# A gated RNN and a GRU on one core: VectorE's bank reads and additions, spread three by three over the half steps

## The chip, the cores and the metric

The kernel runs on one core of one Trainium2 chip. The metric is the device time of one execution in microseconds (us), lower is better. Engines are named as in the profile: PE is TensorE (matmul), PEld its weight loads, DVE is VectorE, ACT is ScalarE, POOL is GpSimd and SP is SyncE, which issues the DMAs.

## The reference, cut to what matters

Two layers, each added to its input `x` of shape (64, 128, 512): 64 sequences of 128 steps and 512 features. Layer 0 is a recurrence that can be written with cumulative sums and is computed as such; the change doesn't touch it. Layer 1 is a GRU with a condition vector per sequence:

```python
vz, vr, vh = video @ C_z + b_z, video @ C_r + b_r, video @ C + b
xz, xr, xh = seq @ W_z, seq @ W_r, seq @ W        # for all steps at once
def step(h, ...):                                  # 128 times, one after the other
    z = sigmoid(xz_t + h @ U_z + vz)
    r = sigmoid(xr_t + h @ U_r + vr)
    hh = tanh(xh_t + r * h @ U + vh)               # (r * h) @ U
    h = (1.0 - z) * h + z * hh
x = x + all h
```

Everything is float32.

## The kernel before, in words

**Layer 0** (the first 690 us or so) goes over 16 groups of four sequences and four blocks of 128 features. It is limited by its matmuls (L232).

**Layer 1** splits the 64 sequences into two *streams* of 32 (`st0`, `st1`) that take turns, so that the matmuls of one stream lie beside the sigmoid, tanh and products of the other. One time step of one stream is a *half step*: the generator `Stream.halves`, driven by `take(n)` along the list `order`. Its parts, in the order of issue:

1. `h` times U_r and U_z (32 PE instructions, L464, `g<-w_s,h`), into the PSUM bank `g`, which already holds the step's x-share.
2. ACT: sigmoid to `r` (L918). DVE, by halves: `rh = r * h` (L922) and its transposition (L923), twice each. ACT: sigmoid to `z` (L927). POOL: `1 - z` (L933) and `(1 - z) * h` (L934).
3. The *middle*: up to two outer products on PE (below), up to three sums on POOL (L810), and on DVE **reads of banks** (`read`), then the deferred transposition of an output (L994).
4. `rh` times U (L464, `g<-w_s,fi`), after that further outer products up to a goal, ACT's tanh (L957), and ACT's copy of the next x-share into `g` (L871).
5. DVE: `hh * z` (L969), plus `(1 - z) * h` (L970), transposition of the new `h` (L974). POOL: `h + x` for the output (L985).
6. The **end** of the half step: one addition of x-sums (`add_c`) and `reads[1]` further reads; SP loads the x-share of two steps later, if it is stored.

**The x-shares** (x times W_z, W_r, W plus the condition) are not computed step by step. For eight time steps of both streams together, a *group*, the products are done by Strassen's scheme in two levels: seven `Outer` operands, each with seven products, 49 products a group, which the planner spreads over 16 half steps (`place`, with `GOALS`). A product is 8 PE instructions (L602). Its banks in PSUM are `r11`, `r12a`/`r12b` (by turns), `r21`, `r22` and `shared`. Within an operand the contents are handed on from bank to bank by ACT (`continued`, L615: r11 to r12, r12 to r21, r21 to r22; L626 copies `shared` to SBUF), and each finished bank is *read* by DVE: `read` adds it to a sum in SBUF (L704, `W<-r,W`); for r12 and r22 the common part is added first in place (L699, `r<-r,x`), as a read of its own. The banks wait in the list `to_read`. An operand gives six reads, a group 42.

Where an operand's sum must still be added to another one, this goes to DVE for operand 4 (`add_c`, L719, `W<-W`, four a group, waiting in `to_add_c`) and to POOL for operand 5 (`add`, L724, four a group). After that SP stores the shares to DRAM (`to_store`, L732) at the beginning of the next half step, and loads them by step and stream (`load_share`, L865).

A product or copy that would overwrite a bank that is not yet read calls `free`, which issues the missing reads first. `read` of operand 5 issues a missing addition of its block first (L694). Instructions marked `pin` stay in program order on their engine, so the order in which `read` and `add_c` are called is the order on DVE; each engine works through its list in order.

How many reads a half step takes is `reads`, which `take` hands over: (2, 2) at the two places where a stream catches up, (4, 1) while the layer fills up, (0, 2) in the last steps, and **(4, 0)** in all half steps between. The middle then takes `max(4, len(to_read) - 2)` reads, as far as there are any; the end takes one addition and no read:

```python
read(reads[0] and max(reads[0], len(to_read) - 2))     # L942, middle
...
add_c()                                                  # L1002, end
read(reads[1])                                           # L1003
```

Of the kernel before, what the change touches and what calls it, by code (L numbers as in the profile page):

```python
# [19 lines left out]
def kernel(  # L20
# [58 lines left out]
    def pin(instruction):  # L79
        return tc.keep_in_program_order(instruction)  # L80
# [484 lines left out]
    class Outer:  # L565
# [121 lines left out]
        def read(self, block, common):  # L687


            (m, j), n, r = block, self.n, self.bank(block)  # L690

            while n in (0, 5) and (m, j) in waiting:
                add(1)
            while n == 5 and (m, j) in waiting_c:  # L694
                add_c()
            if j == 1 and not common:
                if not hasattr(self, "common"):
                    shared_to_copy[0]()
                pin(nc.vector.tensor_tensor(r, r, self.common, ALU.add))  # L699
                return  # L700
            u, s5, c = (acc[:, i, m, j] for i in range(3))
            v1, v21 = v_x[:, j], v_x[:, 2 + j]
            dst, other = ((u, v1), (c, u), (u, u), (s5, v21), (c, s5), (u, u), (c, u))[n]
            pin(nc.vector.tensor_tensor(dst, r, other, ALU.add))  # L704
            unread.discard(r.name)
            if n == 1:
                self.store(c, 0, m, j)
            elif n == 4:
                waiting_c.add((m, j))
                to_add_c.append(lambda: self.add_c(c, u, m, j))  # L710
            elif n == 5:
                waiting.add((m, j))
                to_add.append(lambda: self.add(s5, u, m, j))
            elif n == 6:
                self.store(c, 1, m, j)

        def add_c(self, c, u, m, j):
            waiting_c.remove((m, j))
            pin(nc.vector.tensor_tensor(c, c, u, ALU.add))  # L719
            self.store(c, 0, m, 2 + j)  # L720

        def add(self, s5, u, m, j):
            waiting.remove((m, j))
            pin(nc.gpsimd.tensor_tensor(s5, s5, u, ALU.add))  # L724
            self.store(s5, 1, m, 2 + j)
# [14 lines left out]
    to_read, unread = [], set()  # L740
    to_add, waiting = [], set()
    to_add_c, waiting_c = [], set()
# [23 lines left out]
    def sum_tasks(group):  # L766
# [24 lines left out]
        def halves(d):  # L791
            *ts, op = d
            return [(*[t[:, k] for t in ts], op) for k in range(HC)]

        outer = [
            [(base - 1, ("s", group, i, k), d_) for k, d_ in enumerate(halves(d))]
            for i, d in enumerate(wsums(x_[0][0], x_[0][1], x_[1][0], x_[1][1], s_))
        ]
# [37 lines left out]
    class Stream:  # L836
# [56 lines left out]
        def halves(self, t, filler=None, between=None, targets=lambda: (0, 0), busy=False, reads=(4, 0)):  # L893
# [45 lines left out]
            place(targets()[0], busy)  # L939
            if filler:  # L940
                filler()
            read(reads[0] and max(reads[0], len(to_read) - 2))  # L942
            while deferred:
                deferred.pop(0)()
            if between:
# [52 lines left out]
            if APART <= t + AHEAD < S:  # L998

                pin(nc.gpsimd.tensor_copy(ident.rearrange("p (k b) -> p k b", b=SB), x_of(self, t + AHEAD)))  # L1000
                deferred.append(lambda: pin(nc.vector.transpose(self.output(t + AHEAD), ident)))
            add_c()  # L1002
            read(reads[1])  # L1003
            if t + 2 < S and not direct(self, t + 2) and all((t + 2, q) in stored for q in range(Q)):
                self.load_share(t + 2)
# [226 lines left out]
    for t in range(LEAD + 1, S):  # L1232
        n = order[-1][1] + 1
# [74 lines left out]
    n = 0  # L1308
# [44 lines left out]
```

## Time and profile before

| | |
|---|---|
| time, three runs | 1876.83, 1877.01, 1879.24 us; median 1877.01 |
| profiled execution | 1878.12 us, of it a span of 1876.3 us |
| granted TensorE clock | 0.999 |
| busy in the span | PE 99%, PEld 56%, DVE 80%, POOL 46%, ACT 39% |
| DVE from 1200 to 1600 us | 152 of each 200 us |
| bank reads L704, 128x384 | 0.54 us each |
| additions L719, 128x384 | 60, shortest 0.514, median 0.517, longest 1.050 us |
| output sums L985 | 0.50 us each, waiting mostly for L974 |

A row of a timeline or of the chain has the start in us from the span's start, the length in us, and what it is: engine, line of the kernel, operation, the tile written and the tiles read, and the shape. "x8" says that so many instructions with the same names were merged. In brackets stands how long the engine was idle before, and what ended it. A group of matmuls that has started and waits for its next weights still counts as busy.

### The profile page before, as it was taken

The numbers are of one execution on the slowest core, as the hardware profiler recorded it, in microseconds if no ns is written. First come the engines' busy times: TensorE is split into PE (matmuls) and PEld (weight loads), VectorE is DVE, ScalarE is ACT, GpSimd is POOL, SyncE is SP. The second block draws the span as 40 slices with busy tenths as digits, with TensorE's granted clock in tenths as the row PEclk, the third lists the DMA queues.
The fourth block names the chain that finished last, engine by engine and source line by source line (L and its number), as shares of the span: only waits on it lengthen the run. The fifth ranks groups of instructions, "written<-read, shape, count | busy, mean of one in ns | idle before, by whom it ended". The sixth has DMA issues, their size and how long they took to land.

```text
span 1876.3 us, 62311 instructions
## 1 busy us (share of the span) xinstructions
PE 1864.2 (99%) x24793; PEld 1054.2 (56%) x24793; DVE 1504.9 (80%) x3438; ACT 722.6 (39%) x1888; POOL 865.1 (46%) x1544
## 2 busy tenths in 40 slices
PE   9999999999999999999999999999999999999998
PEld 5444444444444445566666666666666666666567
DVE  5899999999999976777777777777777777777786
ACT  3232223222232233344444444444444444444434
POOL 1233232333333344546556556466565565565650
PEclk9999999999999999999999999999999999999999
DMA  7765433444333241334334344344343343443343
GB/s 181 176 124 119 82 70 73 88 82 83 73 76 65 49 86 29 101 90 142 112 101 142 94 115 133 104 124 126 96 137 109 99 141 101 114 130 96 111 111 78
DMA packets 366754, 195.38 MB, mean 104 GB/s; under 512 B 225332, under 2 KB 352064, under 8 KB 366464
## 3 DMA queue, kind: packets, MB, share of 16 engines
q1 hardware_dynamic: 366280, 191.33, 40.9%
q8 instruction: 195, 3.19, 0.7%
q14 instruction: 95, 0.78, 0.1%
q10 hardware_dynamic: 184, 0.07, 0.0%
HBM read 78.63 MB, written 81.13 MB: 85 GB/s over the span
## 4 chain that ended last, share of the span: by engine, by line
PE 98%; DVE 1%; issue 0%; DMA 0%; ACT 0%; SPq 0%; DVEq 0%; ACTq 0%
PE g L464 36%; PE p L232 35%; PE r L602 14%; PE r12a L602 4%; PE shared L602 4%; PE r12b L602 4%; PE gz L464 1%; PE tp L190 0%; PE pv L464 0%; DMA x<-in_x_dram 0%; DVE W L704 0%; PE g_first L464 0%; DVE fi L923 0%; DVE fi L922 0%; DVE r L339 0%
## 5 line engine op out<-in xcount | busy, mean ns | idle before, releaser
L232 PE MATMUL p<-xT,W 128*128 128x512 f32 (+1 forms) x1560 | 661.9, 586 | 0.0
L232 PEld LDWEIGHTS p<-xT,W 128*128 128x128 f32 x1560 | 293.5, 190 | 361.6 <-issue 359.1
L464 PE MATMUL g<-w_s,h 128*32 128x256 f32 (+1 forms) x8128 | 481.0, 373 | 2.3 <-issue 1.6
L464 PEld LDWEIGHTS g<-w_s,h 128*32 128x32 f32 x8128 | 301.4, 110 | 179.4 <-issue 83.2
L464 PEld LDWEIGHTS g<-w_s,fi 128*32 128x32 f32 x8128 | 222.7, 109 | 113.9 <-issue 55.4
L464 PE MATMUL g<-w_s,fi 128*32 128x128 f32 x8128 | 276.3, 273 | 2.7 <-DVE fi L922 1.3
L922 DVE TENSOR_TENSOR fi<-fi,h 128x64 f32<-128x64 f32 (+1 forms) x494 | 112.3, 227 | 179.3 <-ACT fi L918 178.5
L985 POOL TENSOR_TENSOR h<-h,x 128x128 f32<-128x128 f32 x242 | 121.3, 501 | 232.4 <-DVE h L974 206.8
L314 POOL COPY first<-condT 128x4 f32<-128x4 f32 x64 | 12.6, 196 | 461.8 <-DVE h L386 432.8
L918 ACT ACTIVATE fi<-g 128x128 f32<-128x128 f32 x254 | 70.6, 278 | 327.7 <-PE g L464 308.9
L933 POOL TENSOR_SCALAR fi<-fi 128x128 f32<-128x128 f32 x240 | 72.6, 302 | 236.6 <-DVE fi L922 226.5
L704 DVE TENSOR_TENSOR W<-r,W 128x384 f32<-128x384 f32 x315 | 169.2, 539 | 7.4
L310 ACT ACTIVATE fi<-fi 128x512 f32<-128x512 f32 x64 | 40.4, 631 | 340.6 <-DVE fi L351 340.6
L957 ACT ACTIVATE h<-g 128x128 f32<-128x128 f32 x255 | 70.9, 278 | 236.2 <-PE g L464 236.2
L923 DVE STREAM_TRANSPOSE fi<-fi 128x64 f32<-128x64 f32 (+1 forms) x494 | 122.2, 247 | 22.8 <-PE r12a L602 0.5
L969 DVE TENSOR_TENSOR h<-h,fi 128x128 f32<-128x128 f32 (+1 forms) x264 | 94.9, 359 | 43.8 <-ACT h L957 43.1
L253 POOL TENSOR_TENSOR x<-xT,h 128x512 f32<-128x512 f32 x63 | 122.6, 1946 | 4.9
L934 POOL TENSOR_TENSOR fi<-fi,h 128x128 f32<-128x128 f32 x240 | 110.8, 462 | 20.0
L970 DVE TENSOR_TENSOR h<-h,fi 128x128 f32<-128x128 f32 (+1 forms) x264 | 97.7, 370 | 27.2 <-POOL held L810 0.9
L810 POOL TENSOR_TENSOR held<-held 128x128 f32<-128x128 f32 x240 | 113.7, 488 | 3.1
L602 PE MATMUL r<-w_inner,held 128*32 128x384 f32 x1080 | 114.6, 486 | 0.0
L339 DVE RECIPROCAL r<-r 128x256 f32<-128x256 f32 x60 | 104.2, 1737 | 0.0
(158 smaller groups left out, 2721.5 us busy)
## 6 DMA issues: line engine op xcount, KB each, us to landing
shares<-W SPq DMA_DIRECT2D x240, 192.0 KB, 2.1
xz<-shares SPq DMA_DIRECT2D x480, 48.0 KB, 1.9
whole_v<-shares SPq DMA_DIRECT2D x480, 48.0 KB, 2.0
x2d<-x SPq DMA_DIRECT2D x63, 256.0 KB, 4.2
words<-held SPq DMA_DIRECT2D x240, 64.0 KB, 2.1
out_dram<-o SPq DMA_DIRECT2D x240, 64.0 KB, 1.8
xw_None<-x2d SPq DMA_DIRECT2D x56, 256.0 KB, 3.4
w_rows<-in_L_cond_W_f_dram SPq DMA_DIRECT2D x4, 256.0 KB, 5.7
```

What stands on the lines that cost most here:

```text
L232: nc.tensor.matmul(p[:, tokens], lhsT=W0[:, c, n, k, :], rhs=xT[g][:, k, tokens], start=(k == 0), stop=(k == K - 1),)
L253: nc.gpsimd.tensor_tensor(x2.rearrange("p (t b) -> p t b", b=GB)[:, ts], xT[g][:, c, :].rearrange(f"{layout(g)} -> p t b", b=GB)[:, ts], b ...
L339: pin(nc.vector.reciprocal(r, r))
L464: nc.tensor.matmul(p[q * SB : (q + 1) * SB], lhsT=lhsT(k), rhs=part(wk, q), start=(start and k == 0), stop=(stop and k == len(w) - 1), ski ...
L602: nc.tensor.matmul(self.bank(bank)[q * SB : (q + 1) * SB], lhsT=a[:, q * SB : (q + 1) * SB], rhs=w_, start=start, stop=True, skip_group_ch ...
L704: pin(nc.vector.tensor_tensor(dst, r, other, ALU.add))
L810: pin(nc.gpsimd.tensor_tensor(*a))
L922: pin(nc.vector.tensor_tensor(rh[:, e], r[:, e], h_[:, e], ALU.mult))
L923: pin(nc.vector.transpose(rhT[:, e], rh[:, e]))
L934: pin(nc.gpsimd.tensor_tensor(r, r, h_, ALU.mult))
L970: pin(nc.vector.tensor_tensor(h[:, e], hh[:, e], r[:, e], ALU.add))
L985: nc.gpsimd.tensor_tensor(hh.rearrange("p (k b) -> p k b", b=SB), hT.rearrange("p (k b) -> p k b", b=SB), x_of(self, t), ALU.add,)
```

## The change

Only half steps with `reads == (4, 0)` change. The middle now takes a fixed number of DVE instructions, three, or four if at least six are waiting in both lists together. An addition of x-sums counts as one of them and is issued first; the rest are reads. The end of these half steps has no addition any more. (An addition that `read` itself forces, for operand 5, is not counted.) Half steps with other `reads` are as before.

```diff
@@ halves, the middle
             if filler:
                 filler()
-            read(reads[0] and max(reads[0], len(to_read) - 2))
+            even = reads == (4, 0)
+            if even:
+                n = 3 if len(to_read) + len(to_add_c) < 6 else 4
+                n -= len(to_add_c[:1])
+                add_c()
+                read(n)
+            else:
+                read(reads[0] and max(reads[0], len(to_read) - 2))
             while deferred:
                 deferred.pop(0)()
@@ halves, the end
-            add_c()
+            if not even:
+                add_c()
             read(reads[1])
```

## The prediction

> **What bounds the kernel now.** First the page. Its last lines here are the chain that ended last, as shares of the span by engine.
>
> ```profile
> span 1876.3 us, 62311 instructions
> ...
> PE 1864.2 (99%) x24793; PEld 1054.2 (56%) x24793; DVE 1504.9 (80%) x3438; ACT 722.6 (39%) x1888; POOL 865.1 (46%) x1544
> ...
> PE 98%; DVE 1%; issue 0%; DMA 0%; ACT 0%; SPq 0%; DVEq 0%; ACTq 0%
> ```
>
> TensorE is the chain. VectorE is 80% busy, but its work can only matter where a matmul waits for it, and such a wait hides inside "busy" PE: the group's row simply gets longer. So the second view is the chain piece by piece (start, length, what), for two half steps of layer 1:
>
> ```profile
> 1168.48 0.65 PE r12b L602 x8
> 1169.12 0.65 PE r L602 x8
> 1169.77 1.05 PE g L464 x32
> ...
> 1173.19 0.65 PE r12b L602 x8
> 1173.83 0.65 PE r L602 x8
> 1174.48 0.87 PE g L464 x32
> ```
>
> A half step is `h` times U_r, U_z (1.73 us), two outer products (0.65 each), `rh` times U (0.87), and one product more (at some places two). Undisturbed it takes 4.536 us (the chain's groups of 1.73 start at 1110.77, 1115.31, ... 1133.45). The 1.05 is 0.18 of waiting for `rhT`. I went through the chain from 795.85 to 1794.19 (216 half steps) and took each half step's length less its parts: 7.9 us of waiting, in 49 half steps; the other 167 wait less than 0.02. **So 7.9 us, 0.42%, is all that any rearrangement of VectorE could bring there.**
>
> Third, the timeline (start, length, engine and line), where a wait arises and where it doesn't:
>
> ```profile
> 1302.40 0.46 POOL L985 TENSOR_TENSOR h<-h,x 128x128 f32<-128x128 f32 x1
> 1302.43 0.51 DVE L922 TENSOR_TENSOR fi<-fi,h 128x64 f32<-128x64 f32 x1 [0.24 <-ACT fi L918]
> ...
> 1311.72 0.23 DVE L922 TENSOR_TENSOR fi<-fi,h 128x64 f32<-128x64 f32 x1 [1.27 <-ACT fi L918]
> ```
>
> VectorE's chain to `rhT` (L922, L923, L922, L923) needs 0.9 us after the sigmoid, in which PE has 1.29 us of products. It comes late when GpSimd's L985 runs at the same moment (0.51 for 0.23), and L985 starts when the previous half step's transposition L974 is done and GpSimd's sums L810 are done. Measured from a half step's start, L922 is due at 6.84 (the next half step's 2.30); L985 (0.46) started at 6.43 costs nothing (857.99 in the timeline), at 6.68 it costs 0.09 (923.10), at 6.80 0.21 (1302.40). If L974 ends after 6.95, L922 itself is late: 7.24 (863.42) costs 0.29. It is a window, and not simply "fewer reads is better".
>
> Waits by what the half step before held (reads are L699/L704, 0.54 each; the addition is L719): four reads with an addition L724 and wide sums on GpSimd, 9 half steps, 2.50 us; three reads with the same GpSimd work, 4, 0.85; four reads with other work, 15, 1.62; reads and an addition behind L974, 8, 0.99; an addition among the reads, 10, 0.64; two products that waited for a read, 1.00; one other, 0.32.
>
> The last but one is the fourth view, the chain at 1141:
>
> ```profile
> 1141.73 0.24 DVE fi L923
> 1141.97 0.98 DVE W L704 x2
> 1142.95 0.04 issue
> 1142.99 0.85 PE r L602 x8
> ```
>
> Bank r11 gets its next product right after `rh` times U; its last read was second in VectorE's row, so PE waited 0.50.
>
> **The change part by part.** It adds and removes no instruction. The order on VectorE is fixed by the code, so I followed the counters (`to_read`, `to_add_c`, products placed) half step by half step; for the kernel before this gives the trace's VectorE order in every half step from 795.85 to 1822. For the changed one, from 832.77 on: mid-half-step work of three instructions in 147 half steps instead of 57, of four or five in 25 instead of 65, of one or two in 38 instead of 88. Each term below is such a count times a price from a row.
>
> *Nine heavy half steps* (four reads before wide sums): seven get three reads. The price is then that of the four rows that already have three reads before the same work, 0.21 (1300.14 is one). 2.50 becomes 7 x 0.21 + 0.53 = 2.00: **-0.5**.
>
> *Four reads with other work*, all to three or two: L974 ends 0.48 earlier, by 6.3, L985 falls before L922: **-1.6** (at least -0.8).
>
> *Additions now ahead of the reads.* L719 leaves the place behind L974 and comes right after L923, beside GpSimd's L933/L934. Nine half steps become L719 and three reads: L974 ends near 6.63, inside the window, at about 0.18 each, 1.6, where 0.99 was lost: **+0.6** (-1.0 to +0.9). Those with an addition already in the middle: **+0.3** (0 to +1). L719's price there:
>
> ```profile
> 919.94 0.46 POOL L934 TENSOR_TENSOR fi<-fi,h 128x128 f32<-128x128 f32 x1
> 920.12 0.70 DVE L719 TENSOR_TENSOR W<-W 128x384 f32<-128x384 f32 x1
> ```
>
> 0.70, against a median of 0.517 for all 60; I take 0.6 to 0.7. The Trainium skill's "SBUF — State Buffer", section "Who interferes with whom", speaks against the new place: a VectorE instruction with two SBUF inputs and a GpSimd one that reads SBUF exclude each other for the whole instruction, while one with a single SBUF input (a bank's read) goes undisturbed. By that rule, as an estimate, L719 could wait out all of L934 and end 0.5 later still, and the total below would be 1 us higher.
>
> *Light half steps filled up.* Ten with L724 and three sums on GpSimd had one or two reads and no wait after them; now they have three instructions, three more a late tanh. GpSimd is busy to 6.4 there and L974 moves from 5.9 to 6.5, so L985 starts at 6.6 to 6.7: 13 x 0.10 = **+1.25** (0, or 13 x 0.21 = 2.7).
>
> *Copies that wait for a postponed read.* A read put off to the next half step delays the ScalarE copy (L615, 0.46) that refills its bank, and in ScalarE's order tanh, L871 and the next sigmoid stand behind it. In four half steps the copy waits for the third or fourth instruction: tanh at 5.4 for 4.2, L974 at 6.7 or later: **+0.7** (0 to 1.2). Where it waits for the second, tanh ends at 5.0, when VectorE is only just done with its reads: nothing.
>
> *Products behind such copies.* The seventh product of an operand adds into r21, which the copy r21 to r22 must have read, and the copy needs r22 read. This meets in one half step three times. At 842.49 the reads ran at
>
> ```profile
> 845.67 0.52 DVE L704 TENSOR_TENSOR W<-r,W 128x384 f32<-128x384 f32 x1
> 846.11 0.56 DVE L699 TENSOR_TENSOR r12a<-r12a,x 128x384 f32<-128x384 f32 x1
> 846.27 0.27 PEld L602 LDWEIGHTS r<-w_inner,held 128*32 128x32 f32 x8
> 846.38 0.86 PE L602 MATMUL r<-w_inner,held 128*32 128x384 f32 x8
> 846.70 0.56 DVE L704 TENSOR_TENSOR W<-r12a,W 128x384 f32<-128x384 f32 x1
> ```
>
> After: the addition, the read of r11, then r22's as third, done at 847.35; copy to 847.86; the product at 847.9, not 846.38: +1.53. At 1379.45 r22's read is second (ends 4.18), copy to 4.68, product at 4.75, not 3.89: +0.86. At 1073.29 a product stands between: +0.19. And the 0.50 at 1138.63 grows by an addition ahead of the two reads, +0.66. Together **+3.2** (2.4 to 4.2).
>
> *Loads and stores.* Additions earlier let their stores go earlier; nobody waits for that. Six loads of x-shares (one a group at most) are issued at a half step's start instead of the end of the one two before. Four issues of 0.45 and 1.9 to land give 3.7, needed by L871 at 4.5, and PE feels nothing before the sigmoid at 6.5: 0, by that slack. The last eight products-thin half steps (1794 to 1822) lose an addition behind L974 and gain reads: 0.
>
> Sum: -0.5 - 1.6 + 0.6 + 0.3 + 1.25 + 0.7 + 3.2 = **+4.0 us**. The profiled execution took 1878.12 (span and 1.8 around it), 1.1 over the median of 1877.01, so it would become 1882.1 and the median **1881.0**.
>
> **Rivals.** (1) *Near nothing*: the window is missed more often than hit and the light half steps stay free, as L985 did up to 6.43: the terms of 1.25, 0.7 and 0.6 fall to about a third, +2: 1879; at the bottom of every bound, 1877. For it: prices at the window's edge go from 0 to 0.2 within 0.2 us. (2) *Faster*: the copies' waits are the mechanism to be removed from the sum; if r22's read came in time (if the product at 842.49 starts within 0.2 of `rh` times U, the sign turns), what is left is -2.1 with light half steps free: 1874.5. Against it: the order on VectorE and the chain at 1141, where just such a wait is seen. (3) *Late loads*: if the six loads land over 6.0 into the half step, ScalarE's order holds up the sigmoid; 1 us each is +6 more, 1887. Against it: 2.3 us of slack; for it: SyncE's queue waits for stores. (4) That the change doesn't do what it says: the callers with empty lists at the first steps do nothing, and the rest does split the work into threes; no chance given.
>
> **How the numbers follow.** Forecast 0.55, four fifths of it over 1880.8; near nothing 0.25; faster 0.10, two thirds of it by over 0.2%; late loads 0.10. 0.2% (3.75 us) is about what a measurement of this kernel can tell from no change. Slower 0.44 + 0.10 = 0.54, faster 0.07, same 0.39. Range: bounds of the terms without all falling on one side, +0.3 to +7: 1877.3 to 1884.0.
>
> **What would show it.** Right: on the chain after, a gap of about 1.5 us near 846 and of 0.9 near 1385 (with the small shift by then), with ACT r L615 and DVE W L704 on it; L719 at 0.6 or more on average and right behind L923; groups of 1.05 to 1.10 in other half steps than now, about as many. Wrong: if the product after 845.5 follows at once, or if the `rh` groups are 0.87 nearly everywhere, the time falls by up to 4 us; if ACT g L871 is seen waiting for DMA for over 1 us, the third rival holds.

## The result and the profile after

| | before | changed |
|---|---|---|
| median, 21 runs each | 1877.83 us | 1879.98 us |
| lowest to highest | 1876.83 to 1879.24 | 1879.03 to 1881.77 |
| profiled execution, its span | 1878.12, 1876.3 | 1881.14, 1879.2 |

The ratio is 1.0013, with a 95% interval from 1.0007 to 1.0019: the change makes the kernel 1.3 to 3.6 us slower. 1881.0 was forecast, 1.0 above the measured median. Against its own 1877.0 the forecast was +4.0, and the medians are 2.15 apart, so a good part of what was forecast did not come.

In the changed kernel the lines behind the middle have moved by seven: L957 is L964, L969 is L976, L970 is L977, L974 is L981, L985 is L992, L994 is L1001. First its page:

```profile
span 1879.2 us, 62306 instructions
...
PE 1864.3 (99%) x24793; PEld 1062.6 (57%) x24793; DVE 1495.3 (80%) x3438; ACT 721.0 (38%) x1888; POOL 868.5 (46%) x1544
...
PE 98%; DVE 1%; DMA 0%; ACT 0%; issue 0%; SPq 0%; DVEq 0%; ACTq 0%
```

Nothing on it tells the two kernels apart: PE is the chain with 98%, as before, and is busy for 1864.3 us instead of 1864.2. A loss of 2 us is found only half step by half step. I took the same 216 half steps as the prediction, each by its length less its undisturbed parts. This stretch took 998.34 us before (795.85 to 1794.19), 7.92 of it waiting in 49 half steps; it now takes **1000.77** (797.68 to 1798.45), 10.32 of it waiting in 38: **+2.43 us**. Fewer half steps wait, and they wait longer.

All comparisons below use this stretch, of one profiled execution each, beside the times. It leaves out layer 0, which has the same code in every kernel here, but in the profiled executions ended anywhere from 691.4 to 694.0 us, and the last 82 us. The two profiled spans are 2.9 apart: +1.8 ahead of the stretch, +2.43 in it and -1.4 behind it. The part behind it differs by itself: the run below with the four reads in time has the changed kernel's code there and took 82.6 us, the changed kernel 80.8. One of the 33 runs of the kernel before that four of the experiments are compared with took 3308 us at a granted clock of 0.556; it is left out of their ratios.

The loss is on the chain (start, length, what). After, around the half step that began at 842.49 before:

```profile
847.58 0.44 DVE W L719
848.01 0.93 DVE W L704 x2
848.95 0.23 DVE o L1001
849.18 0.14 issue
849.31 0.47 ACT r L615
...
849.83 0.85 PE r L602 x8
```

VectorE's order is the one that was counted out: the addition L719, then two reads, the second of which is r22's. ScalarE's copy L615 waits for it, and the product of 849.83 for the copy. Between the read's end (848.94) and the copy stand another 0.37 us, which the view puts down partly to the output's transposition L1001; what the copy waits for there isn't clear from the trace. The `rh` group began at 847.34, and 0.87 of work later PE had nothing to do until 849.83, for some 1.6 us. The half step is 1.64 longer than its parts, where it lost nothing before. The second place:

```profile
1384.67 0.06 DVE W L704
...
1385.04 0.55 DVE W L704
...
1385.69 0.47 ACT r L615
...
1386.21 0.85 PE r L602 x8
```

Here r22's read is the second instruction, the copy follows its end (1385.59) within 0.10, and the wait is 0.92. Two more places were forecast, and lose 0.28 and 0.97. In the order of the forecast, the half steps of the four places begin at 844.32, 1381.42, 1074.92 and 1140.26 in the changed kernel. At the fourth no copy stands between: the product waits for r11's read itself, as it did before for 0.50. In the waits view (engine and line, what it waited for: us in all, times, longest) of 820 to 1800, the first row is of before, the second of the changed kernel:

```profile
ACT r L615 <- DVE W L704: 3.9, 3, 1.3
```

```profile
ACT r L615 <- DVE W L704: 23.2, 15, 2.0
```

These 23 us are ScalarE's waits; PE loses 3.8 at the four places, because elsewhere no product needs the copied bank so soon. No wait of `ACT g L871` for a DMA is in that view of the changed kernel.

### The profile page after: what moved, and what is told of

It is laid out like the page before. It is cut to its first block, busy times and chain, and to the rows that moved or that the text cites. A ratio compares the mean times of both kernels' runs of the same rounds, so it can differ in the third digit from the quotient of the medians.

```text
span 1879.2 us, 62306 instructions
## 1 busy us (share of the span) xinstructions
PE 1864.3 (99%) x24793; PEld 1062.6 (57%) x24793; DVE 1495.3 (80%) x3438; ACT 721.0 (38%) x1888; POOL 868.5 (46%) x1544
## 4 chain that ended last, share of the span: by engine, by line
PE 98%; DVE 1%; DMA 0%; ACT 0%; issue 0%; SPq 0%; DVEq 0%; ACTq 0%
PE g L464 36%; PE p L232 35%; PE r L602 14%; PE shared L602 4%; PE r12a L602 4%; PE r12b L602 3%; PE gz L464 1%; PE tp L190 0%; DVE fi L922 0%; PE pv L464 0%; DVE fi L923 0%; DMA x<-in_x_dram 0%; DVE W L704 0%; ACT fi L918 0%; DMA out_dram<-o_last 0%
## 5 line engine op out<-in xcount | busy, mean ns | idle before, releaser
L922 DVE TENSOR_TENSOR fi<-fi,h 128x64 f32<-128x64 f32 (+1 forms) x494 | 110.4, 223 | 203.6 <-ACT fi L918 203.4
L992 POOL TENSOR_TENSOR h<-h,x 128x128 f32<-128x128 f32 x242 | 112.1, 463 | 220.9 <-DVE h L981 206.0
L933 POOL TENSOR_SCALAR fi<-fi 128x128 f32<-128x128 f32 x240 | 91.3, 381 | 246.9 <-DVE fi L922 232.5
L964 ACT ACTIVATE h<-g 128x128 f32<-128x128 f32 x255 | 70.8, 278 | 229.1 <-PE g L464 229.1
L934 POOL TENSOR_TENSOR fi<-fi,h 128x128 f32<-128x128 f32 x240 | 111.2, 463 | 20.0
L976 DVE TENSOR_TENSOR h<-h,fi 128x128 f32<-128x128 f32 (+1 forms) x264 | 90.6, 343 | 30.8 <-ACT h L964 30.1
L977 DVE TENSOR_TENSOR h<-h,fi 128x128 f32<-128x128 f32 (+1 forms) x264 | 93.6, 355 | 26.9 <-DVE h L976 0.9
L810 POOL TENSOR_TENSOR held<-held 128x128 f32<-128x128 f32 x240 | 111.4, 479 | 3.1
```

The costliest lines, as they stand in the source:

```text
L810: pin(nc.gpsimd.tensor_tensor(*a))
L922: pin(nc.vector.tensor_tensor(rh[:, e], r[:, e], h_[:, e], ALU.mult))
L934: pin(nc.gpsimd.tensor_tensor(r, r, h_, ALU.mult))
L977: pin(nc.vector.tensor_tensor(h[:, e], hh[:, e], r[:, e], ALU.add))
L992: nc.gpsimd.tensor_tensor(hh.rearrange("p (k b) -> p k b", b=SB), hT.rearrange("p (k b) -> p k b", b=SB), x_of(self, t), ALU.add,)
```

## The experiments

Two readings were set against each other. The theory: the loss is in four products that wait for a late read, three of them through the copy behind it, and the additions and light half steps are small terms. The rival: the loss comes from the additions' new place on VectorE itself, wherever the reads are.

**Reads alone.** Three or four reads in the middle, additions back at the end and not counted.

```diff
# against the changed kernel
                 n = 3 if len(to_read) + len(to_add_c) < 6 else 4
-                n -= len(to_add_c[:1])
-                add_c()
                 read(n)
...
-            if not even:
-                add_c()
+            add_c()
```

> Three or four reads in the middle, but the additions stay where they were, at the end of the half step, and aren't counted. Theory (the loss comes from reads that the counted additions push into the next half step, so that copies and products wait for them): by the counters no copy and no product waits for a read that it didn't wait for before; the gaps at 844, 1075 and 1381 are gone, the one at 1140 is 0.50 again; only the gain of the even reads is left: 2 to 3 us faster than before (about 1875.3). Rival (the loss comes from the additions' new place beside GpSimd, and evening the reads by itself brings nothing): within 1 us of before.

Measured: 1876.18 (median of 11) against 1877.59 for the kernel before (33 runs); ratio 0.9995 (0.9986 to 1.0004), no difference that times can tell. The stretch took 996.54, **-1.80** against before and 4.2 less than with the whole change. Its chain at the first place:

```profile
844.90 0.87 PE g L464 x32
845.78 0.65 PE r L602 x8
```

The product follows the `rh` group at once. The waits at the second and third place are gone as well, and the fourth is back at its old 0.50. Spreading the reads is worth something; the loss is in what the additions do.

**Additions alone.** The kernel before, with the addition ahead of the reads, on top of them.

```diff
# against the kernel before
+            even = reads == (4, 0)
+            if even:
+                add_c()
             read(reads[0] and max(reads[0], len(to_read) - 2))
...
-            add_c()
+            if not even:
+                add_c()
```

> The additions move to the middle, ahead of the reads, but the reads are as many as before (up to four, or all but two). Theory: no read is postponed, so only the wait at 1140 grows (0.50 to 1.0), and the additions behind L974 stop costing (-1.0) while those beside GpSimd cost some 0.1 each: within 1 us of before. Rival (the place is the loss): 2 us slower or more, with rh groups of 1.05 and above behind most half steps that hold an addition.

Measured: 1880.55 (11 runs), ratio 1.0015 (1.0006 to 1.0023), stretch **+2.53**. Here the theory missed: the place alone costs as much as the whole change, without any read being put off to a later half step. Part of it is the product at the fourth place, which waits 0.98. The larger part is new: seven half steps wait 0.36 to 0.47 where 0 to 0.06 was lost. The timeline of VectorE before one of them:

```profile
1215.24 0.52 DVE L719 TENSOR_TENSOR W<-W 128x384 f32<-128x384 f32 x1
...
1217.21 0.64 DVE L719 TENSOR_TENSOR W<-W 128x384 f32<-128x384 f32 x1
...
1219.14 0.31 DVE L977 STREAM_TRANSPOSE h<-h 128x128 f32<-128x128 f32 x1
1219.37 0.18 DVE L922 TENSOR_TENSOR fi<-fi,h 128x64 f32<-128x64 f32 x1
```

Six instructions stand in this middle: the addition, three reads (left out here), a second addition that the next read, one of operand 5, forces, and that read. The transposition (L977 here) ends at 1219.45, and L922, which should go 6.84 after 1212.12, at 1218.96, follows it directly at 1219.37: 0.41 late. The changed kernel, which counts the addition, waits 0 to 0.16 in these seven half steps. Ahead of the reads, place and count are one trade: uncounted, the addition overfills a half step; counted, it puts a read off.

**Counted, but at the end.** The middle has the changed kernel's number of reads, one less where an addition waits; the addition itself stays behind L974.

```diff
# against the changed kernel
-                n -= len(to_add_c[:1])
-                add_c()
-                read(n)
+                read(n - len(to_add_c[:1]))
...
-            if not even:
-                add_c()
+            add_c()
```

> The additions are counted as in the changed kernel (one read less where one waits), but stay at the end, behind L974. Theory (counting postpones reads, the place ahead of the reads adds 0.5 to each wait): by the counters r22's read is second and not third in the half step at 844, so its gap is 0.9 in place of 1.64; the one at 1075 stays 0.28, at 1140 it is 0.5, at 1381 none, since no read is put off there; additions behind L974 cost 0.2 again in four half steps. In all 0 to 1 us over before. Rival (place alone, as e2's loss suggests): no gap at 844 and 1075, as fast as e1.

Measured: 1877.40 (11 runs) against 1877.92 (15), ratio 0.9997 (0.9988 to 1.0007), stretch -0.34. The chain at the first place:

```profile
845.17 0.91 DVE W L704 x2
...
846.44 0.47 ACT r L615
...
846.96 0.85 PE r L602 x8
```

r22's read is the second of this half step with no L719 ahead of it, and the four places wait 1.18, 0.00, 0.28 and 0.50; in the changed kernel 1.64, 0.92, 0.28 and 0.97; with the reads alone 0, 0, 0 and 0.50. So at these places counting costs 1.96 - 0.50 = 1.46 against the reads alone. The two stretches differ by the same 1.46 (998.00 - 996.54), but only because gains and losses of 0.03 to 0.23 elsewhere cancel out. The place then adds 3.81 - 1.96 = 1.85 at the four places, and 2.77 in the whole stretch. Two expected values were off: 0.9 at the first place became 1.18, since here too the copy starts 0.36 after the read's end (846.08), and the additions behind L974 were to cost 0.2 each in four half steps and cost nothing: with fewer reads ahead of it L974 is done so early that an addition behind it fits.

**The four reads in time.** The changed kernel, with the read that the product needs taken a half step earlier at three places, and at the fourth r11's read first and the addition last.

```diff
# against the changed kernel
+                if (self.s, t) == (1, 45):        # fourth place
+                    i = [b_ for _, b_, _ in to_read].index((0, 0))
+                    to_read.insert(0, to_read.pop(i))
+                    read(3)
+                    add_c()
+                else:
                     n -= len(to_add_c[:1])
                     add_c()
-                    read(n)
+                    read(n + ((self.s, t) in ((0, 13), (0, 38), (0, 71))))
```

> The changed kernel, but in four half steps the order is another: at 839, 1070 and 1375 one read more is taken (that of r22), at 1140 the read of r11 goes first and the addition last. Theory: the four gaps (1.64, 0.28, 0.93, and 0.97 in all at 1140) go, and nothing else moves: 3.2 to 3.8 us faster than the changed kernel, 1 to 1.5 faster than before. Rival (place of the additions, or late loads): within 0.7 us of the changed kernel.

Measured: 1876.18, ratio 0.9994 (0.9985 to 1.0002) to before; the stretch is **3.75 shorter** than the changed kernel's, whose four waits were 3.81 in sum. Four reads in 216 half steps are the whole loss and more: without their waits the change would gain 1.32 in the stretch. Together with the run before, this says how the loss comes about: at the four places the count and the place of the additions make a read late, by 1.46 and 1.85.

**The read that restarts r11 first.** The reads alone, and where the next product is an operand's first, r11's read goes ahead of the others. This was the version that the runs before it pointed to.

```diff
# against "reads alone"
+                blocks = [b_ for _, b_, _ in to_read]
+                if ahead and ahead[0][1].__name__ == "p1" and (0, 0) in blocks:
+                    to_read.insert(0, to_read.pop(blocks.index((0, 0))))
                 read(n)
```

> As e1 (three or four reads in the middle, additions at the end, not counted), and where the next product starts bank r11 anew, r11's read goes first. Theory (a product that waits for a read placed second pays the reads ahead of it): the two waits of 0.50 near 1138 and 1556 go, 1.0 us less than e1; about 2.8 us of layer 1 less than before. Rival (PE was waiting there for its place in the queue, not for the read): the two stay.

Measured: 1876.07 (11 runs) against 1877.06 (15), ratio 0.9994 (0.9985 to 1.0002), stretch 995.63: 0.91 less than with the reads alone, **2.71 less than before**. The fourth place, on the chain:

```profile
1140.09 0.88 PE g L464 x32
1140.97 0.65 PE r L602 x8
```

Both 0.50 waits that the kernel before had are gone. It is the shortest stretch of all versions; by times alone it can't be told from no change.

**Moving the other side of the window.** The kernel before, with the output's sum L985 issued in the next half step behind L933 and L934, so that it can never fall beside L922.

```diff
# against the kernel before
+            while late_sums:                      # behind L933, L934
+                late_sums.pop(0)()
...
-            pin(nc.gpsimd.tensor_tensor(hh..., hT..., x_of(self, t), ALU.add))
+            late_sums.append(lambda: pin(nc.gpsimd.tensor_tensor(...)))
```

> The kernel before, with GpSimd's output sum L985 issued in the next half step, behind L933/L934, and not as soon as L974 is done. Theory (most small waits are L922 sharing its time with L985): L922 runs in 0.23 except where sums L810 reach into it; of the 7.9 us of waits some 2 to 3 go: 1875 to 1876. Rival (L922 is late because VectorE is late, whoever else runs): nothing moves, within 0.5 us of before.

Measured: 1879.41, ratio 1.0009 (1.0000 to 1.0018), stretch +0.87. The theory missed on the total. Some waits with L985 beside L922 did vanish (0.20 to 0.22 in the half steps of 911.66, 985.58, 1059.39 and 1133.23 before), but where a sum L810 takes L985's time the wait stays (at 1300.14 before 0.20, now 0.23), and half steps that had none now lose 0.21 to 0.36. The timeline of one (0.29 now, 0 before):

```profile
1455.63 0.46 POOL L810 TENSOR_TENSOR held<-x 128x128 f32<-128x128 f32 x1
1455.72 0.46 DVE L922 TENSOR_TENSOR fi<-fi,h 128x64 f32<-128x64 f32 x1 [0.29 <-ACT fi L918]
```

GpSimd's sums L810 have moved back by the 0.46 of the output sum and stand where L985 stood: L922 takes 0.46 instead of 0.23. The window belongs to L922, not to L985 alone: a sum L810 there costs about as much.

**Fewer sums on GpSimd in such half steps.** Two instead of three where a sum L724 waits, once on top of the version with r11 first and once on the kernel before.

```diff
+            added = len(to_add)
...
-            take_sums(2 if busy else 3)
+            take_sums(2 if busy or added else 3)
```

> As e6, and in a half step in which GpSimd adds x-sums (L724) it takes two sums L810 at most, not three; the rest follow in the next half steps. Theory (of the waits that are left, most stand behind half steps in which GpSimd's sums run until the next L922): those of 0.14 to 0.33 behind such half steps go, 2 to 2.7 us less than e6, so about 5 us less than before. Rival (these waits come from VectorE's own three instructions): nothing moves against e6.

> The kernel before with only that limit on GpSimd's sums. Theory: the waits of 0.21 to 0.30 behind half steps with an addition and wide sums (3.4 us of the 7.9) shrink by a half or more, those behind four reads stay: 1.5 to 2.5 us less than before. Rival (four reads alone make L974 late): these waits stay within 0.5 us in all.

Measured: 1899.31 (4 runs), ratio 1.0118 (1.0104 to 1.0132), stretch +22.3; and 1908.42 (5 runs), ratio 1.0166 (1.0152 to 1.0180), stretch +27.5. Both theories missed by over 20 us. In the first most of the small waits of 0.14 to 0.33 are gone, in the second those that were 0.26 to 0.30 are mostly 0.16; but some 20 half steps in each now wait 0.5 to 4.3, because a product waits for the sum that is its operand. A row of the waits view of the first (r12b has another like it, the kernel before has neither):

```profile
PE r12a L602 <- POOL held L810: 9.0, 8, 2.4
```

So these small waits go with GpSimd's sums, but its schedule has no slack: moving one sum out of the way costs 25 us against the version with r11 first, where all waiting in the stretch had been 5.1.

## Why the prediction was right, and where it was not

The sign, and the step that carried it, held: products behind late copies were sized at +3.2 and measured **+3.31**. At the second place each step came as worked out (r22's read 4.17 after the half step's start for 4.18, the product 4.79 for 4.75). At the first, the good figure has some luck in it: r22's read ended 4.63 after the start, 0.23 before the 4.86 worked out, and the copy began 0.37 after it, where 0.05 was reckoned. The sum was 1.6 too high, all of it from other terms. By the prediction's own division at 0.2%, the measured +0.13% belongs to "same", given 0.39, and not to "slower", given 0.54. Each in the stretch, forecast first:

| term | forecast | measured |
|---|---|---|
| products behind copies: 842.49, 1379.45, 1073.29, 1138.63 | 1.53, 0.86, 0.19, 0.66 | 1.64, 0.92, 0.28, 0.47 |
| nine heavy half steps | -0.5 | -1.1 |
| four reads with other work | -1.6 | -1.6 |
| additions ahead of reads | +0.6 | **-1.0** |
| additions already in the middle | +0.3 | 0 |
| light half steps filled up | +1.25 | +1.2 |
| copies waiting for a postponed read | +0.7 | +0.6 |
| behind three reads and a third sum | not foreseen | +1.0 |
| sum | +4.0 | +2.4 |

**The mis-sized term is the addition ahead of the reads.** The step said: L719 takes 0.6 to 0.7 beside L933 and L934, so three reads behind it end late and L974 is done near 6.63, inside the window. The timeline after, of the half step before 914.63 and that half step's start:

```profile
913.22 0.72 POOL L933 TENSOR_SCALAR fi<-fi 128x128 f32<-128x128 f32 x1 [0.96 <-DVE fi L922]
913.26 0.52 DVE L719 TENSOR_TENSOR W<-W 128x384 f32<-128x384 f32 x1
913.70 0.55 DVE L704 TENSOR_TENSOR W<-r,W 128x384 f32<-128x384 f32 x1
...
916.14 0.31 DVE L981 STREAM_TRANSPOSE h<-h 128x128 f32<-128x128 f32 x1
...
916.60 0.46 POOL L992 TENSOR_TENSOR h<-h,x 128x128 f32<-128x128 f32 x1 [1.70 <-PE g L464]
916.93 0.23 DVE L922 TENSOR_TENSOR fi<-fi,h 128x64 f32<-128x64 f32 x1 [0.48 <-ACT fi L918]
```

L719 takes 0.52, and the first read starts 0.44 after it. GpSimd's L933 gives way, 0.72 for its usual 0.30. From the half step's start at 910.10 (914.63 less the undisturbed 4.54) the transposition ends at 6.35, not 6.63; L992 starts at 6.50, and L922 keeps its 0.23. The four half steps of this kind (from 914.63 every 73.3 us) went from 0.86 of waiting to nothing. The prediction took its 0.70 from a row in which L934 was already running when L719 came; the new place has L719 coming with L933. The trace of before has one such row, at a half step that the prediction did not use:

```profile
776.23 0.72 POOL L933 TENSOR_SCALAR fi<-fi 128x128 f32<-128x128 f32 x1 [5.27 <-DVE fi L922]
776.27 0.52 DVE L719 TENSOR_TENSOR W<-W 128x384 f32<-128x384 f32 x1
```

The check that it named (L719 at 0.6 or more on average) failed accordingly: 0.54 in the stretch.

The runs add a correction: these four waits are also gone with the reads alone and with the additions counted at the end, where the place is the old one and there are three reads for four, and with the additions alone, where there are four reads behind the addition. One read less clears them, and so does the new place.

**Heavy half steps** were priced at 0.21 by four rows with three reads. Three of the nine (864.11, 937.39, 1010.70) went from 0.29 to nothing: their output sum L992 now starts 0.04 to 0.05 after L922, which keeps its 0.23. In the row of 1302.40, one of the four, L985 started 0.03 ahead of L922. One price for all was the error, and a few hundredths of a us decide it.

**Not foreseen**: three half steps, from 1604.31 every 74 us, went from 0 to 0.29 or 0.30, and the two such half steps ahead of them from 0 to 0.06. The timeline of the first of the three:

```profile
1606.18 0.46 POOL L810 TENSOR_TENSOR held<-x 128x128 f32<-128x128 f32 x1
...
1606.59 0.46 POOL L992 TENSOR_TENSOR h<-h,x 128x128 f32<-128x128 f32 x1
1606.62 0.51 DVE L922 TENSOR_TENSOR fi<-fi,h 128x64 f32<-128x64 f32 x1 [0.65 <-ACT fi L918]
```

A third sum L810 on GpSimd ends as L922 comes, and the output sum behind it starts 0.03 before L922; before the change it started 0.10 after it. The prediction had followed VectorE's counters only; in these half steps it is GpSimd's list that sets when L992 starts.

**Light half steps** came out right in sum (1.2 for 1.25) and wrong in detail: not 13 at 0.10, but four at 0.22 and two at 0.14 and 0.17. None of the six shows the 0.10, which is a mean of passing free and paying most of the 0.2.

**The rivals.** *Late loads* is excluded by the waits view: L871 waits for no DMA. *Faster* is what the run with the four reads in time made of the change: -1.32 in the stretch, where the prediction had worked out -2.1. *Near nothing* had a loss of 2, which is the size that came, but not by its way: it wanted the light half steps, the copies and the additions at a third of their terms, and only the additions fell.

What stays open: no run took a small term (the 1.2, 0.6 or 1.0) away by itself without another loss, so their mechanisms rest on the reading of half steps. The runs narrow them down all the same. The 1.2 and the 0.6 are there, as 1.0 and 0.6, in the run with the four reads in time. They are next to nothing with the reads alone and with the additions counted at the end, and with the additions alone three of their ten half steps wait; so they mostly take the count and the place together. The 1.0 is there, at 1.0 to 1.7, with the reads alone, with the additions counted at the end and with the four reads in time, and not with the additions alone; so it comes from the new number of reads. With r11 first these five half steps wait 0.28 to 0.31, and with one sum less on GpSimd nothing, which fits the reading that the third sum sets the time of L992.

## What to carry to other kernels

Before you even out the work of an engine that isn't the bound, list for each instruction that moves who needs its result next and when: here four bank reads of the 570 in the stretch decided the sign, and the evening-out itself was worth 1.3 to 1.8 us there, too little for the times to show. Where the bounding engine is 99% busy, its waits hide in the length of its groups, so compare the length of each period with its undisturbed parts. And let the instruction that others queue for go first: r11's read at the front brought 0.91 us in the stretch, nearly all of it at the two half steps that had waited 0.50.

## What the runs showed of the hardware that was not expected

When L719 (two SBUF inputs) comes 0.04 us after GpSimd's L933, VectorE's instruction runs its 0.52 undisturbed and GpSimd's is stretched to 0.72, although L933's record starts first. The groups of costly instructions on the page, after:

```profile
L933 POOL TENSOR_SCALAR fi<-fi 128x128 f32<-128x128 f32 x240 | 91.3, 381 | 246.9 <-DVE fi L922 232.5
```

Before, the mean was 302 ns. Of 240 instances 47 now last 0.7, before it was one; of the 18.7 us more nothing reaches PE directly, as 0.2 us is all that anyone is seen waiting for L933. When L933 or L934 is further under way it is the other way round: L719 took 0.59 with L933 0.11 ahead, and 0.70 with L934 0.17 ahead.

Between L922 and the output sum L992 a lead of 0.03 is already enough for GpSimd, so the recorded start alone doesn't tell who waits. In the stretch of the changed kernel, L992 starting 0.01 to 0.04 earlier makes L922 0.51 to 0.52 for 0.23; 0.15 to 0.17 earlier, 0.37 to 0.39; 0.30 to 0.45 earlier, nothing. L992 starting 0.04 to 0.05 later leaves L922 its 0.23 and takes 0.49 to 0.51 itself, for 0.46. The Trainium skill's "SBUF — State Buffer", section "Who interferes with whom", says that such a pair excludes each other and that the order of issue, not the kind of operation, decides who waits. That one of the two is held up agrees with these rows (0.42 more for L933, 0.28 for L922). That it is held up for the whole of the other, as the prediction restates the page, does not, and here the measurement decides: L992 had 0.43 left when L922 started 0.03 behind it, and L922 lost 0.28. The estimate drawn from it in the prediction, that L719 would wait out L934 and the total be 1 us higher, did not come true: in the 47 rows L719 is through before L934 begins.
